# A four-layer graph kernel in fp32: layer 0's gather in two fp32r parts, its counts in one pass, two buffers per one-hot, and layer 1's industry products as a stream that runs two tiles ahead of the loop

## The chip, the cores and the metric

The kernel runs on one core of one Trainium2 chip. The metric is device time in microseconds (us), the median of three runs. All views of a profile come from one profiled execution, whose times are microseconds from the start of its span unless marked ns. Engines are TensorE (PE, with its weight loads as PEld), VectorE (DVE), ScalarE (ACT), GpSimd (POOL) and SyncE (SP, which issues most transfers).

## The reference, cut to what matters

Four layers work on x of 8 batches, 2048 nodes and 64 features, with one 2048 x 2048 adjacency matrix `adj` of which each row is a 0/1 mask divided by its sum. Each layer ends in `x = layernorm(x + layer(x))`.

```python
# layer 0: w_n and b_n are mixes of 16 weights by the node's embedding
x_g = stack(x, A @ x, 2 * A @ (A @ x) - x);  out = einsum('bnki,nkio->bno', x_g, w) + b
# layer 1: nodes n, hyperedges e with membership H[n, e]
h = x @ W;  s = leaky_relu(h @ a_node, 0.2)
alpha = softmax over n of where(H.T > 0, s, NEG);  agg = einsum('ben,bnf->bef', alpha, h)
industry = (adj / deg) @ (x @ W_ind)
all_he = elu(beta * h + (1 - beta) * agg)          # beta = sigmoid(h @ a_gn + agg @ a_ge)
coefs1 = softmax over e of where(H > 0, tanh(elu(agg) @ fcW) @ av, NEG)
g = einsum('bne,benf->bnf', coefs1, all_he)
coefs2 = softmax(attn_scores([industry, g]));  out = coefs2 mix of industry and g
# layers 2 and 3: adj @ x with weights; the normalised adjacency
```

## The kernel before, in words

A tile is 128 nodes; there are NT = 16, and a row of a tile is 8 batches by 64 features (BC = 512). Matmuls that must be exact to fp32 are either f32, or fp32r with one side exact in it (a 0/1 mask) and the other split into a high and a low part, so that two fp32r matmuls add up to the f32 result. The kernel has a short program, which runs on this input, and a general one behind a branch. The short program goes through these stages.

*First product (0 to 155 us).* `first_product` multiplies the masks of `adj` with x and, between its matmuls, takes steps of `memberships`. These build, from H, one-hot matrices `oh01` and `oh23` for the first three memberships of each node, and `S` for the rest, in four quarters q; `store` writes them to DRAM with SP. L415 fills the second half of oh23 a tile at a time; L392 is the PE step before it.

*Layer 0 (155 to about 718).* The loop over j runs eight groups g of `weigh` (L1104 on PE, L1115 on DVE) per tile, with everything else at fixed places between them: `project` (hp, then `h` on ACT and `hs` = h times exp of the score on POOL, L1219), `product` (the second product, L1067), `scaled` (POOL: the mask times a row, and the sum `cs` of the mask's sixteen pieces), `compare`, `first_terms`, `scores`, `gather` (L1224: the sum over nodes that becomes agg, an f32 matmul of the membership copy `md` with `hs`, into the PSUM tile aggp) and `degrees` (L1089: the count of neighbours, an f32 matmul of cs with one column of ones). Row buffers are named homes b0_0 to b0_15 in the pool `own`; each tag has one to three homes. At j = NT, after the last tile's weigh, come `spread` (md again for all tiles), `denominators`, the first steps of `industry_early` and the last two projections and gathers.

*Layer 1.* A first part forms agg, elu(agg), its scores (sep, L582), their sums per node (dnp, L600) and from these hgr, the gate and coefficient inputs. Between them `early` issues the industry product of tile 0, sixteen steps of two fp32r matmuls. Then a loop over t = 0 to 18 works on several tiles at once, in an order written out by hand as a string of turns: u is unit t+1 and v unit t+2 of `units` (gates, two halves gp0/z0/exp0/e0/w0 and gp1/z1/exp1/e1/w1 of the elu, where gp is a PSUM tile with one buffer; red and g), s is unit t, m, o and f are `mix_and_norm` of tiles t-1, t-2 and t-3, p is `industry` of tile t, q of tile t-1. Each p turn issues two steps of the product. `program_order` then binds PE, DVE, ACT and POOL to the order of the text, within the block; SP's transfers are placed by the scheduler. The industry sum of a tile lies in one PSUM bank, tag acc in pool fi with one buffer:

```python
            ind = row("ind", f"ind_{j}")
            nc.scalar.activation(ind, acc, AF.Copy, scale=sdeg)      # L766, turn q.ind
            ...
            nc.vector.scalar_tensor_tensor(                          # L770, turn q.dlt
                dlt, acc, sdeg, g_of[j], op0=ALU.mult, op1=ALU.subtract
```

From t = 16 on, steps of `layer2_steps` are taken in the gaps. Layers 2 and 3 follow as plain loops over the tiles (L1418 with sums a).

Of the kernel before, what the change touches and what calls it, by code (L numbers as in the profile page):

```python
# [18 lines left out]
P = 128  # L19
# [43 lines left out]
def kernel(  # L63
# [35 lines left out]
    nc.vector.tensor_copy(r_(ident_r), ident)  # L99
    ones = const.tile([P, P], F32, tag="ones", name="ones")  # L100
    nc.vector.memset(ones, 1.0)
    eps_t = const.tile([P, 1], F32, tag="eps", name="eps_t")
# [201 lines left out]
    def memberships(pre, ps, pm, fcw_sb, fcb_sb, fcg_sb):  # L304
# [59 lines left out]
        for q in range(NQ):  # L364

            raw = raws.pop(q)
            pT = pre.tile([P, QW], F32, tag="pT", name=f"pT_{q}")
            nc.vector.tensor_scalar(r_(pT), raw, 0.0, None, op0=ALU.is_gt)
            nc.sync.dma_start(lists["pT"][q], pT[0:E])
            yield  # L370
            pf = ps.tile([P, QW], F32, tag="li", name=f"pf_{q}")
            nc.tensor.matmul(
                pf, r_(tri.rearrange("p h e -> p (h e)")), r_(pT[0:E]), start=True, stop=True
            )
            yield
            pfm = raw
            nc.vector.tensor_tensor(pfm, pf, pT, ALU.mult)
            oh01 = pre.tile([P, QW], F32, tag="oh01", name=f"oh01_{q}")
            nc.vector.tensor_scalar(r_(oh01), pfm, order01, None, op0=ALU.is_equal)
            store(q, oh01, 0)  # L380
            oh23 = pre.tile([P, QW], F32, tag="oh23", name=f"oh23_{q}")
            nc.vector.tensor_scalar(r_(oh23[0:64]), pfm[0:64], 3.0, None, op0=ALU.is_equal)
            if q + 1 < NQ:
                load(q + 1)
            S = pre.tile([P, 4, P], F32, tag="S", name=f"S_{q}")
            yield
            for t in range(4):

                j = 4 * q + t
                cols = slice(t * P, (t + 1) * P)  # L390
                sm = ps.tile([P, QW], F32, tag="li", name=f"sm_{j}")
                nc.tensor.matmul(  # L392
                    sm[:, 0:E], r_(pT[0:E, cols]), r_(tri[:, 0, :]), start=True, stop=True
                )
                nc.vector.tensor_scalar(
                    r_(S[:, t, :]), iota[:, 0, :], base3[:, j:j + 1], None, op0=ALU.is_ge
                )
                nc.vector.scalar_tensor_tensor(
                    r_(S[:, t, :]), iota[:, 0, :], end3[:, j:j + 1], S[:, t, :],
                    op0=ALU.is_lt, op1=ALU.mult,  # L400
                )
                yield
                rk = pre.tile([P, 2, E], F32, tag="rk", name=f"rk_{j}")
                for h in range(2):
                    nc.vector.scalar_tensor_tensor(
                        r_(rk[:, h, :]), sm[:, 0:E], base3[:, j:j + 1], pm[:, j, :],
                        op0=ALU.add, op1=ALU.mult,
                    )
                yield
                nc.tensor.matmul(  # L410
                    sm[:, P:2 * P], r_(rk.rearrange("p h e -> p (h e)")), r_(S[:, t, :]),
                    start=True, stop=True,
                )
                yield
                nc.vector.tensor_tensor(  # L415
                    r_(oh23[64:128, cols]), sm[64:128, P:2 * P], iota[64:128, 1, :], ALU.is_equal
                )
            store(q, oh23, 2)
            nc.sync.dma_start(lists["S"][q], S)
            yield  # L420
# [93 lines left out]
    def layer1(  # L514
# [21 lines left out]
        with tc.tile_pool(name="fa", bufs=2) as fa:  # L536
# [10 lines left out]
            with program_order():  # L547
# [13 lines left out]
                early[0](4)  # L561
# [6 lines left out]
                early[0](1)  # L568
# [10 lines left out]
                early[0](2)  # L579
# [17 lines left out]
                early[0](NT)  # L597
# [21 lines left out]
        homes = {"g": (0, 1, 2, 3), "dlt": (4, 5, 7), "ind": (14,), "r": (8, 9, 10),  # L619
# [132 lines left out]
        def industry(j):  # L752

            if j:
                a = mask_tile(mjp, j, "l1")
                acc = ps_acc.tile([P, BC], F32, tag="acc", name=f"ind_{j}")
            else:
                acc = early[1]
            for mt in range(NT):
                if j:  # L760
                    times_mask(acc, a, i_hi, i_lo, mt)
                if mt % 2 == 1:
                    yield "i"
            sdeg = cols_of["sdeg"][:, j:j + 1]
            ind = row("ind", f"ind_{j}")
            nc.scalar.activation(ind, acc, AF.Copy, scale=sdeg)  # L766
            ind_of[j] = ind
            yield "ind"
            dlt = row("dlt", f"dlt_{j}")
            nc.vector.scalar_tensor_tensor(  # L770
                dlt, acc, sdeg, g_of[j], op0=ALU.mult, op1=ALU.subtract
            )
            dlt_of[j] = dlt
            yield "dlt"

        def mix_and_norm(j):
# [4 lines left out]
            ind, g, dlt = ind_of[j], g_of[j], dlt_of[j]  # L781
# [78 lines left out]
        def layer2(j):  # L860
# [27 lines left out]
        g_of, ind_of, dlt_of = {}, {}, {}  # L888
        unit = {j: units(j, g_of) for j in range(NT)}
        mixer = {j: mix_and_norm(j) for j in range(NT)}  # L890
        product = {j: industry(j) for j in range(NT)}
        first = "sx ST gates tau ch0"
        second = "gp0 z0 exp0 ch1 dp t3 e0 w0 gp1 z1 exp1 e1 w1"
        turns = (
            "q.ind u.gp0 u.z0 q.dlt m.xg m.tr0 v.sx m.sT0 v.ST u.exp0 u.ch1 m.fc0 m.tr1 u.dp "
            "o.mult m.sT1 p.i m.th0 f.rstd u.t3 u.e0 p.i o.r m.fc1 v.gates u.w0 o.s u.gp1 p.i "
            "v.tau p.i m.th1 u.z1 s.ga p.i v.ch0 u.exp1 m.sub u.e1 o.centre s.red u.w1 f.x2 p.i "
            "m.df s.g o.sq m.sw o.var p.i p.i"
# [22 lines left out]
        with program_order():  # L921
            run(unit, 0, first)
            run(unit, 0, second)
            run(unit, 1, first)
            for t in range(NT + 3):
                now = {"p": (product, t), "q": (product, t - 1), "u": (unit, t + 1), "v": (unit, t + 2),
                       "s": (unit, t), "m": (mixer, t - 1), "o": (mixer, t - 2),
                       "f": (mixer, t - 3)}
                for turn_ in turns.split():
                    who, what = turn_.split(".")  # L930
                    run(*now[who], what)
                    if t > NT and 0 <= now[who][1] < NT:
                        next(last, None)
# [20 lines left out]
    def layer0(  # L954
# [6 lines left out]
        h_sb, wb, wa, vecs, av_sb, pm, es, hgr, aggp, rden, early = layer1s  # L961
# [3 lines left out]
        homes = {"xT": (0, 1, 2), "xs": (3, 4), "hs": (5,), "y1T": (6, 7), "r": (8, 9),  # L965
# [39 lines left out]
        def scaled(j, h):  # L1005
# [9 lines left out]
            nc.gpsimd.tensor_tensor(cs[:, 0], cs[:, 0], cs[:, 1], ALU.add)  # L1015
            if h == 1:
                nc.gpsimd.tensor_tensor(cs[:, 0], cs[:, 0], msk[j, 0, "s"][1][:, 0], ALU.add)
            msk[j, h, "s"] = ms, cs
# [67 lines left out]
        def degrees(j):  # L1086

            dp = ps_tr.tile([P, QW], F32, tag="tr", name=f"dgp_{j}")
            nc.tensor.matmul(  # L1089
                dp[:, 0:1], msk[j, 1, "s"][1][:, 0], ones[:, 0:1], start=True, stop=True  # L1090
            )
            nc.scalar.copy(deg[:, j:j + 1], dp[:, 0:1])
# [92 lines left out]
        def project(j, h_first=False):  # L1185
# [9 lines left out]
            if j not in mds:  # L1195
                md = tile("md", f"md_{j}", (P, 2, E))
                nc.gpsimd.tensor_copy(md, pm[:, j, :].unsqueeze(1).to_broadcast([P, 2, E]))
# [17 lines left out]
            if not stay:  # L1215
                for t, kept_part in zip((hi, lo), kept_i[j]):
                    nc.sync.dma_start(kept_part, t)
            hss[j] = tile("hs", f"hs_{j}", bufs=1)
            nc.gpsimd.tensor_tensor(  # L1219
                b_view(hss[j]), b_view(h_sb[:, j, :]), bcast(es[:, j, :]), ALU.mult  # L1220
            )

        def gather(j):
            nc.tensor.matmul(aggp, mds[j], hss[j], start=j == 0, stop=j == NT - 1)  # L1224

        def spread():

            mds.clear()
            for q, home in enumerate((1, 2, 3, 10)):
                md = own.tile([P, 4, 2, E], F32, tag=f"b0_{home}", name=f"md4_{q}")  # L1230
                nc.gpsimd.tensor_copy(
                    md, pm[:, 4 * q:4 * q + 4].unsqueeze(2).to_broadcast([P, 4, 2, E])
# [9 lines left out]

        def industry_early():


            a = mask_parts(own, 0, (4, 6, 13, 14), "l1")
            acc = ps_acc.tile([P, BC], F32, tag="acc", name="ind_0")

            def steps():
                for mt in range(NT):  # L1250
                    for part in (y_hi, y_lo):
                        nc.tensor.matmul(
                            acc, r_(a[:, mt, :]), r_(part[:, mt, :]),
                            start=mt == 0 and part is y_hi, stop=mt == NT - 1 and part is y_lo,
                        )
                    yield

            going = steps()

            def go_on(n):  # L1260
                for _ in range(n):
                    next(going, None)

            return go_on, go_on, acc
# [21 lines left out]
        with program_order():  # L1286
# [6 lines left out]
            for j in range(NT + 1):  # L1293
# [4 lines left out]
                for g in range(8):  # L1298
# [9 lines left out]
                    elif g == 1:  # L1308
                        when(j - 1, normed, 1)
                        if j == NT:  # L1310
# [4 lines left out]
                            early.extend(industry_early())  # L1315
                            early.pop(0)(5)
# [20 lines left out]
                    elif g == 5:  # L1337
                        when(j + 1, compare, 1)
                        if j:
# [14 lines left out]
            early[0](3)  # L1354
# [3 lines left out]
    def short_program(top):  # L1358
# [63 lines left out]

        def ln_tiles(pool):
# [6 lines left out]
        with tc.tile_pool(name="l0", bufs=1) as l0, tc.tile_pool(  # L1430
# [15 lines left out]
            with tc.tile_pool(name="l0s", bufs=2) as l0s, tc.tile_pool(  # L1446
# [5 lines left out]
                    y_hi, y_lo, (h_sb, wb, wa, vecs, av_sb, pm, es, hgr, aggp, rden, early),  # L1452
# [697 lines left out]
```

## Time and profile before

| | us |
|---|---|
| median of 3 runs (lowest to highest) | 1318.43 (1313.73 to 1319.35) |
| the profiled execution's own time | 1318.67 |
| its span, first to last instruction | 1316.8 |
| PE busy in the span | 1259.5 (96%) |
| DVE / ACT / POOL busy | 885.0 / 368.4 / 483.5 |
| mean granted PE clock | 0.973 |

The profiled execution lies 0.2 us above the median, so sums are made against it. Busy time of PE is not PE at its peak, since matmuls overlap and their ends are modelled: for PE the distance from start to start is the price of an instruction. "Who waited for whom" names the engine that waited, the line, and what released it, with the total, the number of waits and the longest.

### The profile page before, as it was taken

How to read it: one execution, taken by the hardware profiler on the slowest of the kernel's cores; microseconds unless marked ns; L12 is line 12 of the kernel's file. 1: busy time of each engine (PE TensorE's matmuls, PEld its weight loads, DVE VectorE, ACT ScalarE, POOL GpSimd, SP SyncE). 2: the span in 40 equal slices, each digit the busy share in tenths (PEclk: the TensorE clock that was granted, in tenths of full speed). 3: DMA queues.
4: the chain of work that ended last, by engine and by line, in shares of the span. 5: the costliest groups of instructions: out<-in, count | busy, mean ns of one | idle time of the engine just before them, and what ended most of it. 6: DMA issues, size and time to landing. Idle time of an engine off the chain costs nothing.

```text
span 1316.8 us, 19976 instructions
## 1 busy us (share of the span) xinstructions
PE 1259.5 (96%) x7708; PEld 1002.4 (76%) x7708; DVE 885.0 (67%) x1595; ACT 368.4 (28%) x837; POOL 483.5 (37%) x403
## 2 busy tenths in 40 slices
PE   7999799999999999999999699999998899999996
PEld 6777588888888888888887467777776788888885
DVE  5555268888777877888664568878874655565544
ACT  3000001221122222221222356666664621111111
POOL 1000264444444444444411468888873600000000
PEclk9999799999999999999998589999998999999998
DMA  9887733332333332222272212222220133234551
GB/s 294 238 222 136 215 100 101 107 98 100 107 107 107 106 102 94 94 94 102 81 240 67 103 71 98 96 96 97 81 96 0 50 144 115 109 128 147 176 185 70
DMA packets 100791, 157.22 MB, mean 119 GB/s; under 512 B 12880, under 2 KB 64464, under 8 KB 94672
## 3 DMA queue, kind: packets, MB, share of 16 engines
q1 hardware_dynamic: 98208, 151.65, 35.7%
q10 hardware_dynamic: 2304, 4.20, 0.8%
q8 instruction: 63, 1.03, 0.3%
q0 software_dynamic: 176, 0.02, 0.1%
q14 instruction: 40, 0.33, 0.1%
HBM read 118.08 MB, written 37.76 MB: 118 GB/s over the span
## 4 chain that ended last, share of the span: by engine, by line
PE 89%; DVE 3%; DMA 2%; issue 2%; ACT 2%; POOL 1%; SPq 0%; ACTq 0%; DVEq 0%; POOLq 0%
PE pp L1104 25%; PE a L1418 18%; PE y2p L1067 9%; PE ind L1418 9%; PE y1p L490 8%; PE fc L805 3%; PE df L814 2%; PE gp L705 1%; PE yp L1508 1%; PE try L165 1%; PE trm L165 1%; PE aggp L1224 1%; PE hp L1192 1%; PE sgp L1171 1%; PE red L746 1%
## 5 line engine op out<-in xcount | busy, mean ns | idle before, releaser
L1115 DVE SCALAR_TENSOR_TENSOR r<-pp,emb_sb,r 128x256 f32<-128x256 f32 x512 | 247.4, 483 | 114.8 <-PE pp L1104 100.6
L1104 PE MATMUL pp<-w_sb,xT 64*128 64x256 f32 x1024 | 160.4, 390 | 1.7 <-DVE r L1115 1.7
L1104 PE MATMUL pp<-w_sb,y1T 64*128 64x256 f32 x1024 | 153.5, 376 | 0.0
L1104 PE MATMUL pp<-w_sb,y2T 64*128 64x256 f32 x1024 | 153.5, 376 | 0.0
L1053 POOL TENSOR_TENSOR r<-xs,bn 128x256 f32<-128x256 f32 x32 | 22.7, 731 | 277.2 <-issue 245.4
L1104 PEld LDWEIGHTS pp<-w_sb,xT 64*128 64x128 f32 x1024 | 94.4, 186 | 25.1 <-issue 14.9
L490 PE MATMUL y1p<-x_hi,m 128*128 128x512 f32 x256 | 106.2, 415 | 6.9 <-ACT x_hi L436 6.9
L1104 PEld LDWEIGHTS pp<-w_sb,y1T 64*128 64x128 f32 x1024 | 99.7, 187 | 10.9
L1104 PEld LDWEIGHTS pp<-w_sb,y2T 64*128 64x128 f32 x1024 | 99.6, 187 | 11.0
L1067 PE MATMUL y2p<-y_hi,msk 128*128 128x512 f32 x256 | 103.5, 404 | 0.0
L490 PE MATMUL y1p<-x_lo,m 128*128 128x512 f32 x256 | 103.0, 402 | 0.0
L1418 PE MATMUL ind<-y_hi,mj_l 128*128 128x512 f32 x240 | 101.7, 424 | 0.0
L1067 PE MATMUL y2p<-y_lo,msk 128*128 128x512 f32 x256 | 101.5, 397 | 0.0
L1418 PE MATMUL a<-v_hi,mj_l 128*128 128x512 f32 x256 | 100.1, 392 | 0.0
L1418 PE MATMUL a<-v_lo,mj_l 128*128 128x512 f32 x256 | 99.9, 391 | 0.0
L1418 PE MATMUL a<-y_lo,mj_l 128*128 128x512 f32 x240 | 95.1, 396 | 0.0
L1418 PE MATMUL a<-y_hi,mj_l 128*128 128x512 f32 x240 | 94.9, 396 | 0.0
L1418 PE MATMUL ind<-y_lo,mj_l 128*128 128x512 f32 x240 | 94.6, 394 | 0.0
L1009 POOL TENSOR_TENSOR ms<-msk,srow 128x1024 f32<-128x1024 f32 x32 | 89.8, 2807 | 5.3 <-DVE ms L1022 5.3
L737 POOL TENSOR_TENSOR ez<-ez,coef 128x1024 f32<-128x1024 f32 x32 | 69.8, 2182 | 56.3 <-DVE ez L735 54.3
L1001 DVE TENSOR_SCALAR msk<-adj 128x1024 fp32r<-128x1024 f32 x32 | 63.7, 2024 | 9.2 <-DMA adj<-in_at 9.2
L490 PEld LDWEIGHTS y1p<-x_hi,m 128*128 128x128 f32 x256 | 49.6, 194 | 19.0 <-ACT x_hi L436 6.9
(279 smaller groups left out, 2391.8 us busy)
## 6 DMA issues: line engine op xcount, KB each, us to landing
mj_l<-mask SPq DMA_DIRECT2D x46, 1024.0 KB, 4.9
raw<-in_at SPq DMA_DIRECT2D x32, 512.0 KB, 5.1
adj<-in_at SPq DMA_DIRECT2D x64, 256.0 KB, 3.8
mask<-msk SPq DMA_DIRECT2D x32, 512.0 KB, 4.6
xraw<-in_xn SPq DMA_DIRECT2D x8, 512.0 KB, 4.6
oh<-oh SPq DMA_DIRECT2D x32, 128.0 KB, 2.8
xT<-in_xt SPq DMA_DIRECT2D x16, 256.0 KB, 3.0
xs<-in_xn SPq DMA_DIRECT2D x16, 256.0 KB, 2.9
```

Of the source, the lines that this page charges most:

```text
L165: nc.tensor.matmul(dst, src, ident, start=True, stop=True, is_transpose=True)
L490: nc.tensor.matmul(accs[q][jj], r_(m[:, t, jj * P:(jj + 1) * P]), r_(part[:, mt, :]), start=i + h + t == 0 and part is x_hi, stop=i == 3 a ...
L737: nc.gpsimd.tensor_tensor(by_b(ez), by_b(ez), per_b(coef, 2 * i, 2), ALU.mult)
L805: nc.tensor.matmul(fc[:, h, :], fcw_sb[rs], sT[rs], start=True, stop=True)
L814: nc.tensor.matmul(df[:, b:b + 1], th[:, b % 2, (b // 2) * P:(b // 2 + 1) * P], av_sb, start=True, stop=True,)
L1001: nc.vector.tensor_scalar(r_(m), raws[j][h], 0.0, None, op0=ALU.is_gt)
L1009: nc.gpsimd.tensor_tensor(ms, m, srow[j].unsqueeze(1).to_broadcast([P, 8, P]), ALU.mult)
L1053: nc.gpsimd.tensor_tensor(r[:, 4 * bq * C:4 * (bq + 1) * C] .rearrange("p (h l c) -> p h l c", h=2, l=2), swapped(terms[j]["xs"], bq), bn. ...
L1067: nc.tensor.matmul(acc, r_(msk[j, mt // 8][:, mt % 8, :]), r_(part[:, mt, :]), start=mt == 0 and part is y_hi, stop=mt == NT - 1 and part ...
L1104: nc.tensor.matmul(pp[:, h, pl, :], terms[j][name][rs, 2 * bq + pl], w_sb[rs, k, dq * 4 * C:(dq + 1) * 4 * C], start=k == 0, stop=k == K - 1,)
L1115: nc.vector.scalar_tensor_tensor(rb, ppv[:, :, dd, :], emb_sb[:, j, d:d + 1], rb, op0=ALU.mult, op1=ALU.add)
L1418: nc.tensor.matmul(acc, r_(a[:, mt, :]), r_(part[:, mt, :]), start=mt == 0 and part is hi, stop=mt == NT - 1 and part is lo,)
```

## The change

It has three parts, all in the short program.

1. In layer 0, `hs` of tiles 0 to 14 is split: ACT copies it to fp32r (hs_hi), POOL subtracts (`low_part`, called at g = 5), and `gather` issues two fp32r matmuls with md in fp32r instead of one f32 matmul; tile 15 stays f32. The counts get their sum in a tile `both` in fp32r, and one fp32r matmul with two columns of ones. hs moves to home 15, hs_hi to home 5, hs_lo into the buffer of x1.
2. `oh01` and `oh23` have two buffers each.
3. `industry_early` and the generator `industry` become a class: one stream of 256 steps over all tiles. The ACT read of a finished tile (into ind, in SBUF, three homes) is issued right after its last step, the next tile begins in the same single PSUM bank. 18 steps are issued before unit 0, 14 between the parts of units 0 and 1, and then seven p turns of two steps in every t while any are left. dlt is formed from ind in SBUF. The order of turns is rewritten, and unit 1's first part moves ahead of z1 of unit 0.

```diff
-            oh01 = pre.tile([P, QW], F32, tag="oh01", name=f"oh01_{q}")
+            oh01 = pre.tile([P, QW], F32, tag="oh01", name=f"oh01_{q}", bufs=2)
...
-            oh23 = pre.tile([P, QW], F32, tag="oh23", name=f"oh23_{q}")
+            oh23 = pre.tile([P, QW], F32, tag="oh23", name=f"oh23_{q}", bufs=2)
...
-                early[0](NT)
+                products.go_on(3)
                 dn = ps_tr.tile([P, NT, 2, B], F32, tag="tr", name="dnp")
...
+        products.mask_of = lambda j: mask_tile(mjp, j, "l1")
+        ind_of = products.sums
+
+        def mix_and_norm(j):
...
+            ind, g, dlt = ind_of[j], g_of[j], row("dlt", f"dlt_{j}")
+            nc.vector.scalar_tensor_tensor(dlt, ind, 1.0, g, op0=ALU.mult, op1=ALU.subtract)
             yield "dlt"
...
         turns = (
-            "q.ind u.gp0 u.z0 q.dlt m.xg m.tr0 v.sx m.sT0 v.ST u.exp0 u.ch1 m.fc0 m.tr1 u.dp "
-            "o.mult m.sT1 p.i m.th0 f.rstd u.t3 u.e0 p.i o.r m.fc1 v.gates u.w0 o.s u.gp1 p.i "
-            "v.tau p.i m.th1 u.z1 s.ga p.i v.ch0 u.exp1 m.sub u.e1 o.centre s.red u.w1 f.x2 p.i "
-            "m.df s.g o.sq m.sw o.var p.i p.i"
+            "u.gp0 p.i m.dlt m.xg p.i f.rstd m.tr0 v.sx s.ga m.sT0 u.z0 u.exp0 m.fc0 o.mult m.tr1 "
+            "v.ST v.gates m.sT1 u.ch1 p.i o.r m.th0 u.dp u.t3 u.e0 u.w0 s.red o.s u.gp1 m.fc1 "
+            "m.th1 p.i s.g u.z1 p.i p.i v.tau m.sub u.exp1 p.i o.centre o.sq u.e1 v.ch0 m.df f.x2 "
+            "m.sw u.w1 o.var"
         )
...
             run(unit, 0, first)
-            run(unit, 0, second)
+            run(unit, 0, "gp0 z0 exp0 ch1 dp t3")
+            products.go_on(8)
+            run(unit, 0, "e0 w0 gp1")
             run(unit, 1, first)
+            products.go_on(6)
+            run(unit, 0, "z1 exp1 e1 w1")
...
-                dp[:, 0:1], msk[j, 1, "s"][1][:, 0], ones[:, 0:1], start=True, stop=True
+                dp[:, 0:2], r_(msk[j, "sum"]), r_(ones_r), start=True, stop=True
...
+            hss[j] = tile("hs", f"hs_hi_{j}"), hs
+            nc.scalar.copy(r_(hss[j][0]), hs)
+
+        def low_part(j):
+            if j < NT - 1:
+                hi, hs = hss[j]
...
+                lo = tile("x1", f"hs_lo_{j}", bufs=1)
+                nc.gpsimd.tensor_tensor(r_(lo), hs, hi, ALU.subtract)
+                hss[j] = hi, lo
...
         def gather(j):
-            nc.tensor.matmul(aggp, mds[j], hss[j], start=j == 0, stop=j == NT - 1)
+            for part in hss[j]:
...
+                a, b = (mds[j], part) if j == NT - 1 else (r_(mds[j]), r_(part))
+                nc.tensor.matmul(
+                    aggp, a, b, start=j == 0 and part is hss[0][0], stop=j == NT - 1
+                )
...
+        class industry:
...
+            def rows(self, own, ps_acc, hi, lo):
+                for j in range(NT):
+                    a = self.mask_of(j)
+                    acc = ps_acc.tile([P, BC], F32, tag="acc", name=f"ind_{j}")
+                    for mt in range(NT):
+                        times_mask(acc, a, hi, lo, mt)
+                        if mt == NT - 1:
+                            ind = own.tile(
+                                [P, BC], F32, tag=f"b0_{(14, 11, 15)[j % 3]}", name=f"ind_{j}"
+                            )
+                            nc.scalar.activation(
+                                ind, acc, AF.Copy, scale=cols_of["sdeg"][:, j:j + 1]
+                            )
+                            self.sums[j] = ind
+                        yield
```

## Prediction

> **What bounds the kernel now.** I read the page's busy shares first, then busy time by stage, then who TensorE (PE) waited for, then the timeline at the places that the change touches.
>
> The stage view (start:end, length, busy us of PE, weight load, VectorE (DVE), ScalarE (ACT), GpSimd (POOL), granted PE clock, DMA) shows layer 0 (155 to 695) and the layer 1 loop (768 to 1010) full on PE, and a thin stretch between them at a low clock:
>
> ```profile
> 155.00:695.00 540.00, 537.32 (x4172) 448.85 (x4173) 414.31 (x769) 102.42 (x208) 245.93 (x222) 1.00 0.33 110
> ...
> 735.00:768.00 33.00, 19.47 (x52) 11.37 (x51) 20.83 (x38) 13.32 (x37) 22.10 (x15) 0.56 0.21 83
> ...
> 780.05:990.00 209.95, 209.28 (x1034) 150.06 (x1033) 166.84 (x254) 142.10 (x365) 165.18 (x114) 1.00 0.27 96
> ```
>
> The last row is thirteen iterations of the loop (t=2 to 14), 16.15 us each. So PE time taken out of layer 0 or out of an iteration comes off the end, and PE time moved into 720 to 768 can be nearly free. PE's own waits (total, times, longest):
>
> ```profile
> PE gp L705 <- DVE ez L735: 13.5, 4, 4.3
> PE sm L392 <- DVE oh L415: 7.0, 4, 5.8
> ```
>
> The first lies wholly in that thin stretch. The timeline gives the prices: a gather in layer 0 and the matmul after it; the last product of a tile and its reader in the loop; the wait of 5.8 us.
>
> ```profile
> 431.13 1.10 PE L1224 MATMUL aggp<-hs,md 128*128 128x512 f32 x2
> 432.17 0.70 PE L1104 MATMUL pp<-w_sb,xT 64*128 64x256 f32 x4
> ...
> 860.60 0.40 PE L1418 MATMUL ind<-y_lo,mj_l 128*128 128x512 f32 x1
> ...
> 861.03 0.69 ACT L766 ACTIVATE ind<-ind,sdeg 128x512 f32<-128x512 f32 x1 [1.79 <-PE ind L1418]
> ...
> 141.37 0.69 DVE L1001 TENSOR_SCALAR msk<-adj 128x1024 fp32r<-128x1024 f32 x1 [8.27 <-DMA adj<-in_at]
> 142.09 0.29 DVE L415 TENSOR_TENSOR oh<-sm,iota 64x128 fp32r<-64x128 f32 x1
> 142.44 0.42 PE L392 MATMUL sm<-tri,pT 64*128 64x64 f32 x1 [5.83 <-DVE oh L415]
> ```
>
> Read starts, not lengths: the f32 gather holds PE 1.04 us; products (fp32r) follow each other every 0.229 us, their ends modelled 0.17 us past the next start.
>
> **What the skill says.** "FP8 and Floating Point Precision", TensorE Precision Notes: true FP32 takes four passes through the array. The trace agrees: dp's f32 and fp32r matmuls (L725, L726) hold PE 1.09 us together, so 0.86 for f32 against 0.23, near four to one. "TensorE: Matmul & The Clock Gate", Part 1: the clock is half or full, decided over windows of about 3.4 us of activity. The trace agrees: 0.50 in 726.6 to 736.6 and in 740.2 to 767.3, where PE idles or runs one-column work. "PSUM — Partial Sum Buffer", Engine vs sequencer instructions: matmuls start in program order, so one that waits blocks all behind it. The trace fits (PE stands at gp while later work is ready).
>
> **Part 1, gather and counts.** Each of 15 gathers becomes two fp32r matmuls. The nearest row is y2p after hp: first product 0.34 us to the second, then 0.23, so 0.57 against 1.04: 0.47 saved. Fourteen lie in full layer 0: -6.6 us (0.40 to 0.55 each: -5.6 to -7.7); the fifteenth lies in the thin stretch and the last stays f32. A count (L1089) holds PE 0.31 us; one fp32r pass of few columns takes 0.11 (sx, L648) to 0.22 (sm, L392), 0.15 saved, times 16: -2.4 (-1.4 to -3.2). Sum **-9.0**.
>
> Added: an ACT copy (0.58) and a POOL subtraction (1.27, as L1013) per tile. POOL in layer 0 runs without a gap from 413.1 to 429.6 and then idles 18.5 us; the subtraction comes after the counts, near 424, and its matmul at 431. It pushes what follows on POOL (scaled, y1) by 1.3 us; y1 is needed 13 us later. ACT's copy ends near 417, its next work is at 421.6. The subtraction writes into x1's buffer, free once trx has read it (421.9) and the store to kept, issued at 413.0, has landed; hs lies in sq's home, read by 410. So these cost nothing while that idle stands. md and both are the same instructions in fp32r form; ones_r is one small copy at the start.
>
> At the end this cover is gone. ACT now has the copy of hs_14 (waits POOL to 712.7, ends 713.3) ahead of the xT_15 copy, which ran at 711.46: sgp, hp and h of tile 15 are 1.9 us late. POOL's hs_15, which before stood 0.75 us for gather 14, has a home of its own now, so the last gather is **+1.2** (0 to +2).
>
> **Part 2, two buffers per one-hot.** L415 waits for neither buffer nor stores: DVE stands at the layer 0 mask ahead of it, which waits for its load. DVE's and SP's order here is as before, so this wait stays, and no DVE wait for an oh store is in the trace. **0** (-0.5 to 0).
>
> **Part 3, the stream.** Products keep one PSUM bank, and a tile's first product now follows the last of the tile before, with the ACT read between. Price: last start to modelled end 0.40, read 0.69, two handovers of 0.05, less the 0.23 spacing: **0.95 us**, during which PE does nothing else.
>
> *Before unit 0.* go_on(3) runs step 16 of tile 0, then two steps of tile 1, ahead of dnp, which feeds rec, hgr and the chain to the gates. At half clock a product takes 0.43: 0.95 + 4 x 0.43 = **+2.7** (+1 to +3).
>
> *From gp of unit 0 (733.8) to the start of t=2 (780.07).* Before: 13.5 + 13.5 + 19.4 = 46.3. After, first leg: dp done at +2.5, sixteen products half of them cold 5.3, gp1 at +8.0 instead of +7.6, sx and gates of unit 1 ahead of z1 (+2), twelve products (2.7), tile 1's read ahead of exp1, e1 done: 16.4. Second leg (t=0): unit 1's gates and d lie ready, so z0 no longer waits for POOL; the chain gp, z0, exp, e0, gp1, z1, exp, e1 with its neighbours gives 11.6, about PE's 10.2. Third (t=1): full clock, 15.2 + 0.95. Sum 44.1: **-2.2** (-6 to +3).
>
> *Loop, t=2 to 14.* Seven p turns of two steps replace eight. PE per iteration falls by two steps, 4 x 0.229 = 0.92: 13 x 0.92 = -11.9. A tile is eight p turns, so its boundaries drift through the seven places. No other PE work stands between places 1 and 2, nor between 4, 5, 6 and 7; of fourteen boundaries eight fall there (t=1, 4, 5, 6, 9, 12, 13, 14), seven in this stretch: 7 x 1.0 = +7.0 (ACT may be late with tanh). Elsewhere fc, dp or df cover the read. **-4.9** (-11.9 to 0). dlt now reads SBUF, same length. From t=15 on: 14 steps against 16, then the mixers' chain as before: 0. SP's mask loads still go out when tile j-2 ends, a tile early; tile 1's four parts (1 MB) load near 700, where DMA is 0.13 busy: 0.
>
> Is an iteration of 15.2 still PE's? Gp has one buffer. From gp0 to gp1 PE has 8.0 us of work; the chain through z0 2.45, exp 1.12 with mult, gates and r (2.2) before e0 1.23 takes 6.7. From gp1 to the next gp0 PE has 7.1; fc1, th1, sub, centre, e1 take 6.0. DVE's sum is 13.7 us and POOL's 13.1. So yes, with about 1.2 us to spare in each half.
>
> **Sum.** -9.0 + 1.2 + 0 + 2.7 - 2.2 - 4.9 = -12.2 against the profiled execution's 1318.67 (span 1316.8 and 1.9 around it): **1306.5**. The median shown, 1318.43, stands 0.2 below, so it serves for both.
>
> **Rivals.**
> *Boundaries are hidden and the early products warm the clock:* loop -10, thin stretch -2 instead of +0.5, the rest as above: -19.8, about 1299. For it: 33 us of idle, cold PE; against: PE cannot pass a waiting product.
> *The gain is given back:* the loop's boundaries eat all (loop 0, sum -7.3, 1311.4), and the stretch takes its upper ends besides (+6 in place of +0.5: 1317), or gathers wait 0.5 us each for POOL (+7 on the main sum: 1313.5). For it: DVE and POOL would be some 88% busy in an iteration; against: the slack worked out above.
> *Slower:* the loop becomes a latency chain over the single gp buffer. DVE is in order, e1 stands behind sub and centre, and a boundary's ACT read delays exp1. Layer 0 and the stretch leave -7.3, so +6.6 needs +13.9 over 14 iterations: it decides from a period of 17.1, PE idle 1.9 in each. At 17.5 the time is 1330. Against: the 1.2 spare.
> *It does not do what it says:* true of part 2.
>
> **How the numbers follow.** About 0.5% (6.6 us) is what a measurement can tell from no change. Main forecast, 1302 to 1311.5: 0.56. Hidden and warm, below 1302: 0.18. Given back, 1311.5 to 1325: 0.18. Slower chain: 0.08. Faster 0.74, same 0.18, slower 0.08. The range of 1297 to 1317 takes in the first two and most of the third.
>
> **What would show it.** Layer 0's tile period 33.98 us falls to 33.4, gather slots to 0.57. PE's waits for oh L415 stay near 7. Loop periods alternate 15.2 and 16.2, with PE waiting near 1 us for ind's ACT read at t=1, 4, 5, 6, 9, 12, 13, 14. Wrong if every iteration is near 16 or PE waits at gp in each, or if the aggp row shows PE waiting for POOL.

## The result, and the profile after

The changed kernel takes 1327.7 us (median; 1319.35 beside it for the kernel before): ratio 1.0082, 95% interval 1.0062 to 1.0102. It is slower by 0.8%, where 1306.5 and "faster" were forecast. (The ratio is estimated from all the runs together; the quotient of the two medians would be 1.0063.) The profiled execution has a span of 1325.5 us against 1316.8. The kernel before took 1313.3 to 1322.4 us in its eleven runs and the kernel after 1322.2 to 1333.4, and a profile shows one run of each. Starts of the same instruction in both traces split the difference:

| stretch | before | after | change | forecast |
|---|---|---|---|---|
| start to first y2p | 155.1 | 154.1 | -0.9 | 0 |
| first y2p to first denp (layer 0) | 545.2 | 537.3 | -7.9 | -9.0 |
| denp to gp of unit 0 | 33.5 | 37.3 | +3.8 | +3.9 |
| gp of unit 0 to gp of unit 3 | 46.3 | 43.3 | -3.0 | -2.2 |
| gp of unit 3 to gp of unit 15 (twelve iterations of the loop) | 193.8 | 203.4 | **+9.6** | **-5.0** |
| gp of unit 15 to first u (tail) | 43.8 | 49.7 | **+5.9** | 0 |
| first u to the end | 299.2 | 300.3 | +1.1 | 0 |

(The loop's -5.0 is the forecast's thirteen iterations without t=14: 12 x -0.92 and six boundaries of 1.0.) Everything ahead of the loop went about as forecast. The loop and the tail are the miss.

The stage view of the kernel after, with the columns as before (PE, weight load, DVE, ACT, POOL, granted clock, DMA):

```profile
155.00:691.00 536.00, 533.25 (x4188) 449.72 (x4188) 418.41 (x775) 112.48 (x225) 274.81 (x236) 1.00 0.34 111
...
772.00:975.00 203.00, 186.69 (x911) 128.73 (x910) 183.79 (x240) 127.72 (x337) 151.43 (x107) 1.00 0.26 85
```

Layer 0 is still full on PE. The loop is not: PE was busy all the time before, now 187 of 203 us, and DVE, busy for 12.8 us of each iteration before (166.84 over thirteen), is busy for 184 us, which is 15.3 of each 16.95. Whom PE waits for in the whole kernel (total, times, longest):

```profile
PE gp L708 <- DVE ez L738: 17.1, 16, 3.1
...
PE ind L1407 <- ACT ind L1433: 7.0, 9, 0.8
PE sm L394 <- DVE oh L417: 6.7, 4, 5.5
PE sgp L1163 <- ACT xT L1158: 2.9, 1, 2.9
```

The first line lay wholly in the thin stretch before. Now twelve of its 16 waits, 11.5 us, lie in the loop, eleven of them at gp1 and one, of 0.2 us, at gp0: gp has one buffer, and e0 comes late out of DVE. The second is the forecast's boundary stall (nine, 0.8 us each, six of them in the loop). The third is part 2's wait, untouched. The fourth is the end of layer 0.

The chain of work that ended last was 89% PE and 3% DVE before, as shares of the span. Now (the shares shown add up to 48%) it goes through DVE as well:

```profile
PE 30%; DVE 12%; ACT 4%; issue 2%; POOL 0%; DVEq 0%; ACTq 0%; POOLq 0%
```

Why is DVE late? Its groups in the loop (790 to 970 us; busy, mean ns of one, idle before), first of the kernel before, then after:

```profile
L770 DVE SCALAR_TENSOR_TENSOR dlt<-ind,sdeg,g 128x512 f32<-128x512 f32 x11 | 8.2, 745 | 0.0
...
L831 DVE SCALAR_TENSOR_TENSOR r<-s,r 128x512 f32<-128x512 f32 x11 | 7.5, 682 | 0.0
...
L826 DVE SCALAR_TENSOR_TENSOR r<-dlt,r 128x512 f32<-128x512 f32 x11 | 7.5, 681 | 0.0
```

```profile
L764 DVE SCALAR_TENSOR_TENSOR dlt<-ind,g 128x512 f32<-128x512 f32 x10 | 20.8, 2083 | 0.0
L815 DVE SCALAR_TENSOR_TENSOR r<-s,r 128x512 f32<-128x512 f32 x10 | 16.7, 1671 | 0.0
L810 DVE SCALAR_TENSOR_TENSOR r<-dlt,r 128x512 f32<-128x512 f32 x11 | 14.4, 1309 | 0.0
```

dlt, centre (L815) and r (L810) are the same work on the same shapes, and take 2.08, 1.67 and 1.31 us instead of about 0.7. No other long group of DVE grew by more than 0.01 us. Together that is 3.0 us in each iteration (against 0.68: 1.40 + 0.99 + 0.63), and the profile books it as busy, not as a wait. The timeline of one iteration after shows what stands beside them (start, us, engine):

```profile
873.10 1.91 POOL L740 TENSOR_TENSOR ez<-ez,coef 128x1024 f32<-128x1024 f32 x1 [1.82 <-DVE ez L738]
...
873.47 2.08 DVE L764 SCALAR_TENSOR_TENSOR dlt<-ind,g 128x512 f32<-128x512 f32 x1
...
879.84 1.04 POOL L695 TENSOR_TENSOR d<-h,sig 128x512 f32<-128x512 f32 x1
...
880.13 1.29 DVE L810 SCALAR_TENSOR_TENSOR r<-dlt,r 128x512 f32<-128x512 f32 x1
...
881.35 1.21 DVE L738 SCALAR_TENSOR_TENSOR ez<-gp,d 128x1024 f32<-128x1024 f32 x1
...
882.62 0.30 PEld L708 LDWEIGHTS gp<-agg,oh 128*128 128x128 f32 x2 [2.09 <-DVE ez L738]
```

POOL's operation ends at 875.01 and dlt at 875.55; POOL's next ends at 880.88 and r at 881.42. Each time DVE finishes 0.54 us after POOL, as if it had waited for POOL to end and then done its own work. Then e0 follows late; the weight load of gp1 stands 2.1 us for it, and PE itself 1.3.

The Trainium skill, "SBUF — State Buffer", Who interferes with whom, has the rule: DVE's second pair of SBUF ports is GpSimd's only one; a DVE instruction with two SBUF inputs and a GpSimd instruction that reads SBUF exclude each other, and whichever starts first makes the other wait in full. An operand in PSUM does not count. The trace agrees: all twelve dlt of the loop end 0.55 us after the w beside them, while DVE's g (L751), of whose two inputs one is in PSUM, takes 0.67 us beside the other w (883.08 in this iteration, within the w of 882.64). Before, dlt read acc in PSUM and g in SBUF, and stood where POOL was idle (863.98, when POOL had nothing from 864.01 to 866.61); after, it reads ind and g, both in SBUF, and stands beside w. Both had changed.

The kernel before had the same conflict with the roles exchanged, and its profile showed it. One r and the w beside it in the kernel before, then POOL's multiplication w in the loop, before and after:

```profile
866.38 0.68 DVE L826 SCALAR_TENSOR_TENSOR r<-dlt,r 128x512 f32<-128x512 f32 x1
866.61 2.22 POOL L737 TENSOR_TENSOR ez<-ez,coef 128x1024 f32<-128x1024 f32 x1 [2.61 <-DVE ez L735]
```

```profile
L737 POOL TENSOR_TENSOR ez<-ez,coef 128x1024 f32<-128x1024 f32 x22 | 49.5, 2248 | 32.6 <-DVE ez L735 32.6
```

```profile
L740 POOL TENSOR_TENSOR ez<-ez,coef 128x1024 f32<-128x1024 f32 x21 | 40.0, 1904 | 35.1 <-DVE ez L738 35.1
```

The same operation took 0.34 us more before, because DVE's r and centre had started 0.23 and 0.16 us ahead of it and POOL waited. The new order of turns reversed who comes first. POOL had time to spare (its instructions add up to 13.0 us of 16.15 before); DVE had little.

### The profile page after: what moved, and what is told of

Same layout as the page of the kernel before. It is cut to its first block, busy times and chain, and to the rows that moved or that the text cites. A ratio compares the mean times of both kernels' runs of the same rounds, so it can differ in the third digit from the quotient of the medians.

```text
span 1325.5 us, 19957 instructions
## 1 busy us (share of the span) xinstructions
PE 1254.7 (95%) x7692; PEld 998.5 (75%) x7692; DVE 921.5 (70%) x1596; ACT 374.7 (28%) x852; POOL 515.2 (39%) x418
## 5 line engine op out<-in xcount | busy, mean ns | idle before, releaser
L1096 PEld LDWEIGHTS pp<-w_sb,y1T 64*128 64x128 f32 x1024 | 99.9, 187 | 10.7
L1407 PE MATMUL ind<-y_hi,mj_l 128*128 128x512 f32 x224 | 92.9, 415 | 6.2 <-ACT ind L1433 6.2
L1407 PE MATMUL ind<-y_lo,mj_l 128*128 128x512 f32 x224 | 88.9, 397 | 0.0
L740 POOL TENSOR_TENSOR ez<-ez,coef 128x1024 f32<-128x1024 f32 x32 | 61.6, 1925 | 55.9 <-DVE ez L738 55.9
L1407 PEld LDWEIGHTS ind<-y_hi,mj_l 128*128 128x128 f32 x224 | 43.0, 192 | 29.0 <-issue 11.4
```

The costliest lines, as they stand in the source:

```text
L740: nc.gpsimd.tensor_tensor(by_b(ez), by_b(ez), per_b(coef, 2 * i, 2), ALU.mult)
L1096: nc.tensor.matmul(pp[:, h, pl, :], terms[j][name][rs, 2 * bq + pl], w_sb[rs, k, dq * 4 * C:(dq + 1) * 4 * C], start=k == 0, stop=k == K - 1,)
L1407: nc.tensor.matmul(acc, r_(a[:, mt, :]), r_(part[:, mt, :]), start=mt == 0 and part is hi, stop=mt == NT - 1 and part is lo,)
```

## The experiments

Three theories for the loop. PORT: the above, the 3 us of hidden waits in DVE's in-order queue set the period. BANK: the one product bank, with ACT's read at each tile boundary. ORDER: the latency of the new turns over the one gp buffer (the forecast's slower rival). "Loop" is gp of unit 3 to gp of unit 15; ratios are to the kernel before, run beside each (its medians there were 1316.8 to 1318.1 us).

| kernel | ratio (95%) | median us | loop us | gp 15 to u |
|---|---|---|---|---|
| before | 1 | 1319.35 | 193.8 | 43.8 |
| after | 1.0082 (1.0062 to 1.0102) | 1327.7 | 203.4 | 49.7 |
| one_input_dlt | 0.9986 (0.9970 to 1.0001) | 1315.4 | 194.4 | 45.4 |
| one_input_all | 0.9964 (0.9947 to 0.9981) | 1311.9 | 190.5 | 45.6 |
| no_boundary | 1.0031 (1.0015 to 1.0048) | 1320.8 | 202.4 | 44.5 |
| dlt_moved | 0.9986 (0.9964 to 1.0008) | 1314.8 | 192.4 | 47.6 |
| reorder | 0.9981 (0.9967 to 0.9995) | 1314.4 | 194.2 | 45.3 |
| part1_only | 0.9972 (0.9957 to 0.9987) | 1314.0 | 193.8 | 44.2 |
| part2_only | 0.9997 (0.9980 to 1.0013) | 1319.1 | 193.8 | 43.9 |
| part3_only | 1.0124 (1.0086 to 1.0161) | 1334.3 | 203.1 | 47.6 |
| tile14_f32 | 1.0066 (1.0043 to 1.0088) | 1327.6 | 203.1 | 47.3 |
| tail_exp_first | 1.0050 (1.0018 to 1.0082) | 1327.3 | 203.3 | 50.5 |
| combined | 0.9970 (0.9953 to 0.9986) | 1314.0 | 191.6 | 45.4 |
| combined_spread | 0.9941 (0.9922 to 0.9960) | 1311.2 | 191.7 | 42.6 |

### One SBUF input for dlt

```diff
-            nc.vector.scalar_tensor_tensor(dlt, ind, 1.0, g, op0=ALU.mult, op1=ALU.subtract)
+            nc.vector.tensor_reduce(dlt, ind.unsqueeze(2), AX.X, ALU.add)
```

> The kernel after, with dlt computed by a tensor_reduce over a last axis of one element, from ind alone: the same place in the order, the same shape, about the same length (0.67 us), but one SBUF input instead of two; the subtraction of g is left out. Loop: from gp of tile 3 to gp of tile 15, 203.4 us in the kernel after and 193.8 before. Theory PORT (a DVE operation with two SBUF inputs waits until the POOL operation beside it ends, and DVE's queue, with 3 us of such waits in each iteration, is what sets the loop's 16.95 us): dlt falls from 2.08 to 0.7 us, the loop to 187 to 195 us, the total to 1310 to 1319, since PE's 15.3 us come next. Theory BANK (the one product bank, read by ACT between two tiles, makes the loop long): dlt's length does not matter, loop 201 to 204, total within 2 us of the kernel after. Theory ORDER (the latency of the new order over the one gp buffer, gp to z to exp to e): dlt stands in front of z0, so a part is gained, 0.5 us in each iteration: loop 197, total 1321.

dlt takes 0.67 us, the loop falls by 9.0 us to 194.4, and the ratio from 1.0082 to 0.9986, some 13 us. BANK is out as the main cause, and the gain is more than the 6.4 us that ORDER allowed.

### One SBUF input for all three

```diff
-            nc.vector.scalar_tensor_tensor(r, dlt, 0.5, r, op0=ALU.mult, op1=ALU.add)
+            nc.vector.tensor_reduce(r, dlt.unsqueeze(2), AX.X, ALU.add)
...
-            nc.vector.scalar_tensor_tensor(
-                b_view(r), bcast(s), -1.0 / C, b_view(r), op0=ALU.mult, op1=ALU.add
-            )
+            nc.vector.tensor_reduce(r, r.unsqueeze(2), AX.X, ALU.add)
```

> The kernel after, with dlt, r and centre (the three long DVE operations of the loop with two SBUF inputs) each computed by a one-input tensor_reduce of the same shape; the second terms are left out. PORT: DVE's time in an iteration falls by 3.0 us (dlt 1.4, centre 1.0, r 0.6), PE is the bound again, the loop falls to 184 to 190 us and the total to 1305 to 1313. BANK: loop 201 to 204, total unchanged. ORDER: at most 1 us in each iteration, loop 192 to 197, total 1316 to 1321.

The three groups of this kernel in the loop, at the places that they had after, and then its loop in the stage view:

```profile
L764 DVE TENSOR_REDUCE dlt<-ind 128x512 f32<-128x512 f32 x11 | 7.4, 676 | 0.0
...
L810 DVE TENSOR_REDUCE r<-dlt 128x512 f32<-128x512 f32 x10 | 6.8, 676 | 0.0
L815 DVE TENSOR_REDUCE r<-r 128x512 f32<-128x512 f32 x10 | 6.8, 676 | 0.0
```

```profile
776.89:967.35 190.46, 185.62 (x915) 131.02 (x914) 154.30 (x240) 129.24 (x339) 146.80 (x107) 0.99 0.27 92
```

All three take 0.68 beside the same POOL operations: the length was the second SBUF input, not the place alone. DVE falls to 154 us, 12.9 an iteration, and PE is the bound again: none of its waits at gp is left in the loop. The order of turns is that of the kernel after, so ORDER by itself costs nothing. The loop, 190.5, ends 0.5 above what PORT gave. Its periods from t=2 on are 15.3, 15.2, 16.3, 16.3, 16.3, 16.8, 15.2, 16.2, 15.3, 15.2, 16.2, 16.3: long at t=4, 5, 6, 9, 12 and 13, just where the forecast had put its boundaries, and at t=7, where the clock fell to half for 3.4 us. The forecast's account of PE was right; what it left out was the port.

### No wait between two industry tiles

```diff
-                                ind, acc, AF.Copy, scale=cols_of["sdeg"][:, j:j + 1]
+                                ind, hi[:, j, :], AF.Copy, scale=cols_of["sdeg"][:, j:j + 1]
```

> The kernel after, with ACT's copy of a finished industry tile reading y_hi (SBUF) instead of the product's PSUM bank: the products' sums are not used, and the first product of the next tile waits for nobody. PORT: DVE's queue still sets 16.7 us in each iteration, so only what the tile boundaries add beyond that goes: loop 199 to 203, the tail 2 to 3 us shorter (exp of the last unit no longer stands behind that copy), total 3 to 7 us below the kernel after. BANK: PE's work of 15.3 us sets the period, loop 184 to 190, total 13 to 20 us below the kernel after. ORDER: loop 200 to 203.

The loop stays at 202.4, with dlt at 2.08 us as after. With the boundary waits gone, the loop is about as long as in the kernel after, which excludes BANK; PORT and ORDER had both expected this. The total is some 7 us lower. Its profile, of the slowest of its runs, has the tail at 44.5 against 49.7, which is more than the 2 to 3 us expected there, and denp to gp of unit 0 at 39.9 against 37.3.

### dlt moved, and nothing else

```diff
-            "u.gp0 p.i m.dlt m.xg p.i f.rstd m.tr0 v.sx s.ga m.sT0 u.z0 u.exp0 m.fc0 o.mult m.tr1 "
+            "u.gp0 p.i m.xg p.i f.rstd m.tr0 v.sx s.ga m.sT0 u.z0 u.exp0 m.fc0 o.mult m.dlt m.tr1 "
```

(with the instruction moved accordingly in `mix_and_norm`)

> The kernel after with dlt, whole, moved in the order from right after gp (POOL at w1 there) to right after mult (POOL at rstd there, beside which mult takes 0.69 us). Nothing else is changed. PORT: dlt falls from 2.08 us to 0.7 to 1.2, loop 187 to 197 us, total 1311 to 1321. BANK: unchanged, loop 203, total 1327. ORDER: z0 starts about 1.4 us earlier but gates, r and e0 stand behind dlt instead: loop 200 to 203, total 1324 to 1327.

Its dlt in the groups of the loop, and in the timeline with the POOL operation beside it:

```profile
L791 DVE SCALAR_TENSOR_TENSOR dlt<-ind,g 128x512 f32<-128x512 f32 x11 | 7.6, 690 | 0.0
```

```profile
872.43 1.99 POOL L830 TENSOR_TENSOR rstd<-var,mhalf 128x8 f32<-128x8 f32 x1
872.81 0.69 DVE L791 SCALAR_TENSOR_TENSOR dlt<-ind,g 128x512 f32<-128x512 f32 x1
```

One instruction in another place, the same arithmetic: the loop falls from 203.4 to 192.4 us, the total by some 13 us, and the kernel is level with the one before. BANK and ORDER had it nearly unchanged. POOL's rstd does not hold dlt up; it has 8 elements per partition to read. But rstd is itself longer than in the kernel after (1.99 against 1.67): here mult, which also has two SBUF inputs, had started 0.22 us ahead of it. r and centre still wait in this kernel (1.34 and 1.60 us on average over the loop).

### All three moved

```diff
-... o.mult m.dlt m.tr1 v.ST v.gates m.sT1 u.ch1 p.i o.r m.th0 ...
+... o.mult o.r m.dlt m.tr1 v.ST v.gates m.sT1 u.ch1 p.i m.th0 ...
-... u.z1 p.i p.i v.tau m.sub u.exp1 p.i o.centre o.sq u.e1 ...
+... u.z1 v.tau u.exp1 p.i p.i o.centre m.sub p.i o.sq u.e1 ...
```

> The kernel after with dlt and also r moved to right after mult (POOL at rstd), centre moved ahead of sub (POOL not yet at the next d), and exp of z1 put ahead of the last three product steps in ACT's order, so that it never stands behind the copy of a finished industry tile. PORT: the waits of all three DVE operations go, the loop falls to that of the kernel with three one-input operations or below: 186 to 191 us; the tail to df of tile 15 falls by 3 to 5 us from 47.7; total 1304 to 1311. If DVE-first now makes POOL wait and POOL becomes the bound: loop 192 to 196, total 1312 to 1316.

A miss for the first expectation: the loop is 194.2, not below 191. centre fell to 0.81 us, but r and dlt, now behind each other, run past rstd into POOL's next operations (1.07 and 1.48 us on average from 790 to 950 us). The total of 1314.4 and the loop lie in the second expectation's ranges, but POOL is not the bound: its instructions add up to 13.3 us of each 16.2. The tail to df fell as expected, to 43.2. Iterations without a boundary take 15.2 to 15.4 at best; those with one up to 17.8: ACT's copy of ind stands behind exp there, and PE's longest wait for it is 1.4 us instead of 0.8. The waits changed places.

### The parts one by one

part1_only is the kernel before with layer 0's edits, part2_only with `bufs=2` for oh01 and oh23, part3_only with the stream and the new turns.

> The kernel before with layer 0's edits alone (gather in two fp32r parts, counts in one pass), one-hots and layer 1 as before. If layer 0 gains its 8.8 us up to the denominators and loses 3.8 us at its end (xT of tile 15 behind the hs_hi copy of tile 14, and TensorE at half clock after that idle): last split gather 5 us earlier, loop 193.8 us as before, total 4 to 6 us below the kernel before. If the loss at the end of layer 0 were due to the new stream's mask loads there instead: 8 to 9 us below.

> The kernel before with two buffers for each one-hot and nothing else. If DVE stands at the layer 0 mask, which waits for its load, and not at a buffer: PE's wait for the one-hot stays at 5.8 us, the total within 0.1% of the kernel before. If the buffer or a store held it: that wait falls below 1 us, the total 3 to 5 us lower.

> The kernel before with the stream of products and the new turns alone; layer 0 and the one-hots as before. PORT: the loop's loss needs nothing of layer 0: dlt 2.08 us, loop 202 to 205 us (193.8 before), tail to df of tile 15 47 us (41.7 before), less the 3 us gained from gp of unit 0 to unit 3: total 10 to 14 us above the kernel before. If part of the loop's loss came from buffers that part 1 takes (hs_lo, hsf): loop below 200, total less than 6 us above.

Part 1 is worth 0.28% (3.7 us): just under the 4 to 6 expected, and far from 8 to 9. Its trace gains 7.2 us up to denp, less than the 8.8 expected, and loses the 3.8 from there to the gather of tile 14 (17.9 us after denp against 14.1), so that loss belongs to part 1 itself. Part 2 is worth nothing, and PE's wait is still there; PE's waits in part2_only:

```profile
PE sm L392 <- DVE oh L415: 6.6, 4, 5.5
```

Part 3 alone gives the loop of 203.1 us, so nothing of part 1 takes part in it; its total is 16 us up, above the expected 10 to 14. The product of the three ratios, 1.0093, lies within the interval of the kernel after.

### The end of layer 0

```diff
-            if j == NT - 1:
+            if j >= NT - 2:
                 hss[j] = hs,
                 return
```

(and the same bound in `low_part` and `gather`)

> The kernel after with the gather of tile 14 left in f32 like that of tile 15, so that ACT has no hs_hi copy ahead of the xT copy of tile 15 and POOL no subtraction. Theory of the end of layer 0 (xT late by 1.9 us, and the idle drops the TensorE clock to half for sgp, hp and the gathers, which gives the other 2 us): from the first denominators to the last split gather 17.9 us falls to 14 to 15.5 (before: 14.2), PE's wait for xT from 2.9 to about 1 us, total 2 to 4 us below the kernel after. If the clock there falls for another reason (one-column denominators and few products in flight, as before): 16.5, total about 1.5 below.

In the kernel after, ACT and PE at this place:

```profile
703.97 0.62 ACT L1218 CAST hs_hi<-hs 128x512 fp32r<-128x512 f32 x1 [1.22 <-POOL hs L1211]
704.49 0.58 ACT L1158 COPY xT<-trx 128x512 f32<-128x512 f32 x1
...
705.12 1.87 PE L1163 MATMUL sgp<-wa,xT 128*128 128x4 f32 x8 [2.92 <-ACT xT L1158]
```

Without that copy sgp follows its transposes by 1.74 us as before (3.58 after), and tile 14's gather comes 15.3 us after denp. But the clock was at half from 704.4 to 711.2 all the same, the last gather comes only 1.0 us earlier (19.6 us after denp against 20.65), and the total does not move. The wait went; the clock did not follow: 13.7 us of the stretch from denp to the last gather ran at half, as in the kernel after (13.6; before 6.8).

### The tail

```diff
+                order = turns
+                if t == NT - 2:
+                    order = turns.replace("u.z1 p.i p.i ", "u.z1 ").replace("u.exp1 ", "u.exp1 p.i p.i ")
```

> The kernel after with one move in one iteration, that of the last unit: exp of its second half is put ahead of the product steps before it, so that on ACT it no longer stands behind the copy of industry tile 14. If that copy is what made the tail longer: from gp of tile 15 to the last df 47.7 us falls to 43 to 44.5 (before: 41.7), total 3 to 5 us below the kernel after. If the tail is longer because the products have run out and TensorE falls to half clock: 46.5 to 47.7, total within 1 us.

exp came 2.3 us earlier after gp (11.0 instead of 13.3) and e1 1.8, but red of the last unit, which needs e1, stands at 26.3 us in both, and the last df at 48.4: that exp was not the cause, and the result lies on the rival's side. Stage rows from gp of unit 15 to about u, of the kernels before, after, and with exp first:

```profile
974.00:1018.00 44.00, 37.50 (x182) 26.45 (x182) 25.05 (x30) 24.40 (x57) 19.41 (x17) 0.95 0.10 36
```

```profile
975.00:1025.00 50.00, 42.12 (x177) 28.99 (x176) 29.23 (x30) 24.16 (x59) 24.45 (x18) 0.80 0.07 24
```

```profile
977.00:1027.00 50.00, 42.12 (x171) 28.30 (x169) 27.77 (x29) 23.47 (x56) 23.68 (x18) 0.76 0.06 21
```

The mean clock is 0.95 before and 0.80 and 0.76 here. Over all the kernels the tail is longer the more of it runs at half clock, with small exceptions: 43.8 us with 4.5 at half before, 44.2 with 7.2 (part1_only), 44.5 with 12.9 (no_boundary), 47.6 with 17.4 (dlt_moved), 49.7 with 20.6 after, 50.5 with 24.4 (tail_exp_first). The kernel without boundary waits, with its shorter tail, fits into this row. But no run changed the clock alone: what drops it, and how much of the longer tail it makes, is not settled.

### A version that beats both

```diff
-... p.i o.r m.th0 u.dp ... u.z1 p.i p.i v.tau m.sub u.exp1 p.i o.centre o.sq u.e1 ...
+... p.i o.r m.th0 u.dp ... u.z1 p.i p.i v.tau o.centre m.sub u.exp1 p.i o.sq u.e1 ...
```

combined is dlt_moved with this, the tail's order and tile 14 in f32; combined_spread also has `m.xg f.rstd m.tr0 p.i v.sx` in place of `m.xg p.i f.rstd m.tr0 v.sx`.

> The kernel after with dlt moved to right after mult, centre moved ahead of sub, exp ahead of the products in the iteration of the last unit, and the gather of tile 14 in f32. PORT: centre's wait falls from 1.0 to 0.2 us besides dlt's, the loop to 189 to 192 us (192.4 with dlt alone moved), the tail to df to 42.5 to 44.5 us, total 1307 to 1312, below both kernels. If the waits only change places (as when r was moved too: loop 194): loop 193 to 195, total 1313 to 1315.

> The same with the second product step of an iteration put behind the transposes of g, so that a tile boundary between the first two steps has 0.5 us of other PE work to cover part of ACT's read. BANK (as a second-order cost): three of the loop's boundaries lose 0.5 us each, total 1 to 2 us below the kernel with the moves alone. If sT and fc, which follow those transposes, were what the first half waits for: no gain, within 1 us.

combined has centre at 0.74 us and a loop of 191.6, as expected, and a tail to df of 43.3, as expected too, but a total of 1314.0: it missed its 1307 to 1312. In its profile gp of unit 0 to gp of unit 3 takes 46.9 us where the kernel after took 43.3, with 13.8 us of it at half clock instead of 2.9; combined_spread has the same there (46.5). Why is open. combined_spread is the fastest kernel here, 0.6% below the one before (ratio 0.9941). Its loop:

```profile
773.96:965.65 191.69, 186.23 (x914) 131.00 (x914) 159.07 (x240) 129.76 (x339) 154.15 (x107) 0.99 0.28 91
```

That is 191.7, no shorter than combined's: the spread did nothing for the loop. Between the two profiles its lead is 5.7 us, of which 1.5 lie ahead of the first y2p and 2.8 in the tail, where 7.5 us run at half clock against 10.7. (From denp to the last gather matmul it took 17.0 us against 18.6 with the same instructions, 6.8 at half clock against 10.3, but at gp of unit 0 only 0.5 of that is left.) The intervals of the two ratios overlap, so what the spread itself is worth is open.

## Why the prediction was wrong

**The failed step** is the paragraph "Is an iteration of 15.2 still PE's?" with the clause ahead of it, "dlt now reads SBUF, same length". The length is 2.08 us, not 0.7, and "DVE's sum is 13.7 us" became 16.6 (the lengths of all its instructions in an iteration, which overlap a little; 13.9 in the kernel before), with r and centre stretched by the new turns. By halves: from gp0 to gp1 dlt and r lost 2.0 us where 8.0 less 6.7 left 1.3 to spare, and PE stood at gp1 in eleven of twelve iterations, up to 1.3 us in each. From gp1 to the next gp0 centre lost 1.0 where 1.1 was to spare, and PE hardly waited. The loop missed by 14.6 us (-5.0 against +9.6); with the three operations short it is 190.5, so 12.9 of these are the port's, and most of the rest is the half clock at t=7. The prediction added up durations from the kernel before and never asked which of them depend on what runs beside; the page's mean for w, 2.18 us (2.25 in the loop) where six undisturbed ones take 1.90, was the hint at hand. Two runs show it from two sides, the second input taken away (190.5) and the instruction moved (192.4).

**The slower rival** had the right outcome, a loop near 17 us with PE waiting at gp, but in part by luck. Its own sum "decides from a period of 17.1", and at the 16.95 measured it gives only +4 us (14 x 0.8 less 7.3); the 7.0 us of the tail and what follows it, which it did not foresee, made the rest. Its mechanism was half right as well. DVE in order, yes; ACT's read at a boundary delaying exp1, no: without those reads the loop is 202.4. And the order alone, without the port, gives 190.5.

**The tail**, "from t=15 on: 0", cost 5.9 us to u and 1.1 beyond. The prediction took for granted that the last mixers run as before; 20.6 us of the tail ran at half clock where 4.5 had. part3_only loses 3.8 there, so it comes mostly with part 3. Which step of the new order brings it is open.

**Layer 0's** -9.0 became -7.9. The term that was too large is the gather: 0.64 us in two parts where 0.57 was taken from y2p, so 0.39 saved, just under the range given; a count fell from 0.31 to 0.20 instead of 0.16. These two make 7.3 of the 7.9. The POOL subtraction and the ACT copy cost nothing in the full stretch, as said: no PE wait for POOL appears at aggp.

**Denp to gp of unit 0** was +3.8 against +1.2 and +2.7, right in sum and wrong in both parts: the last gather came 4.2 us later, since 6.8 us more at half clock were added to the wait of 1.9 us (1.8 measured), and from there to gp it was 0.4 us shorter. That the sum came out is luck: one_input_all, whose program is the same up to there, took 40.6 us from denp to gp of unit 0 where after took 37.3, with 24.0 us at half clock against 14.1. The Trainium skill, "TensorE: Matmul & The Clock Gate", Part 1, says that the window which sets the clock runs freely, so that it depends on where work falls in it. The runs fit: the same instructions from denp to the last gather matmul took 20.1, 18.6 and 17.0 us in tile14_f32, combined and combined_spread, with 13.7, 10.3 and 6.8 us at half clock.

**Part 2 at zero, the stretch to unit 3 at -2.2** (-3.0) and the boundary stalls (0.8 us of PE's waiting, nine times; six places in the loop as listed) held.

## What to carry to other kernels

When an edit moves an operand from PSUM to SBUF, or reorders DVE against POOL, list the DVE instructions with two SBUF inputs and what POOL does beside each: if POOL's operation reads as much as here, the one that starts second waits for the other, and the profile books that as busy time with no wait shown. A group whose mean stands well above its shape's usual length is the sign; put such instructions beside POOL work that reads little (here rstd), or where POOL has run dry, and let the engine with slack come second. Sum an engine's queue with durations that hold in the new order, not with those of the old one.

## What the runs showed of the hardware

- A 128x512 DVE operation with two SBUF inputs ended 0.55 us (0.54 in the rounded lines above) after the POOL operation beside it, wherever in that operation it had started: 2.08 us beside w (1.91), 1.29 beside d (1.04), in the kernel after. With one SBUF input, in the same places, it took 0.68.
- The other way round, POOL's w ended 1.76 us after the DVE operation that had started just before it, in all 24 cases of the loop before (2.25 us on average, 1.90 undisturbed).
- POOL's rstd (128x8, 1.7 to 2.0 us) did not hold such an operation up (0.69, from 0.18 us after its start on), though the rule that the Trainium skill gives in "SBUF — State Buffer", Who interferes with whom, has the pair taken for the whole instruction. Here the measured number decides. rstd does wait itself: where mult had started 0.22 us ahead, it took 1.99 us instead of 1.67. Whether the recorded length of rstd is its time at the port was not tried.
- A two-part fp32r gather took 0.64 us from start to start of the next work, against 1.04 in f32.
